# A Mamba and attention hybrid on one core: softplus on copied, wide tiles, and layer-norm statistics moved from VectorE to ScalarE

## The chip, the core and the metric

The kernel runs on one core of a Trainium2 chip. The core has five engines that each work through their own list of instructions in order: TensorE (PE; its weight loads have a row PEld), VectorE (DVE), ScalarE (ACT), GpSimd (POOL) and SyncE (SP, which here only issues transfers). They meet at semaphores. The metric is the device time of one execution in microseconds (us).

## The reference, cut to what matters

The input x is 8 images of 384 channels and 32 x 32 = 1024 positions, in float32. Two layers follow each other for each image.

```
# layer 0, for the image read forward and backward
u, z   = split(x_norm @ in_proj.T)
u      = silu(causal_conv4(u))
dt, B, C = split(u @ x_proj.T)                 # 24, 16 and 16 columns
delta  = softplus(dt @ dt_proj.T + dt_bias)
h[t]   = exp(delta*A) * h[t-1] + (delta*u) * B # 16 states for each channel
y      = (sum over states of h*C + u*D) * silu(z)
x      = x + res * (scale*(fwd + bwd) @ out_proj.T + sigmoid(conv3x3(x_norm)) * x_norm)
# layer 1, tokens t of 384 channels
t = t + causal_attention(layernorm(t))
t = t + feed_forward(layernorm(t))             # exact GELU, Kronecker-factored weights
```

The change concerns three places of it: the softplus that makes `delta`, the product `delta*u`, and the mean and variance of the two layer norms.

## The kernel before, in words

**Tiles and stages.** A half of an image is 512 positions; a tile of 128 x 512 is 128 channels over a half. An image takes four scan steps (`STEPS`: direction and half), and each step 12 units (3 blocks of 128 channels by 4 groups of states), so 48 units an image. In a unit the 128 partitions hold 32 channels by 4 states, and the four quarters of the channel block lie beside each other. One unit in `scan` is: GpSimd multiplies `hs = du * br` over 128 x 2048; ScalarE makes four tiles `da = exp(delta * A)` of 128 x 512 into five PSUM buffers (`DAS`); VectorE runs four scans over them and, in 8 of 12 units, multiplies each by `cr`; in the other units (`POOL_C`) the scans end in `hs` and GpSimd does one product with `cr`; TensorE sums the states with `sel` into the PSUM tile `y`. A small ScalarE copy (`carry`) keeps the state where a half ends.

**What feeds the scans.** `norm_in` loads x, normalizes it into the tile `xn` and projects it; `raw_gate` projects the gate from the same `xn`; `conv_tokens` makes `uc`; `prepare` (line 954) then works for one or two steps at a time. It makes `xd` by a matmul, and for each channel block and step a matmul `rates` of 128 x 512 into PSUM; `store` (line 989) takes the softplus of it, out of PSUM into a transit tile `tmp`, multiplies `uc` by it in place, and stores both to DRAM (`dd`, `db`), from which the scans load them replicated (`dl`, and `du` in a buffer of `hs`). `uc` itself has been stored to `ud` before. Tiles `tmp` are 15 shared transit buffers of 128 x 512 (`TMP`): inputs, projections on their way to DRAM, loads of `ud`, `yd`, `zs` and `lx`, and outputs. There are 17 calls of `prepare`: three for the first image, two for each other.

**Layer 1.** `project` (line 1147) sums the layer-0 result of 128 tokens in PSUM and copies it into `t1`. `token_norm` (line 1175) makes the statistics of one to four tiles of 128 tokens x 384 with `bn_stats` and `bn_aggr` on VectorE, then `rstd` and `-mean*rstd` on ScalarE; `normed` applies them. `attention` and `feed_forward` each begin with it, and `attention` ends each tile with a VectorE operation that adds its result to `t1`. That is 128 tiles of statistics in all, in 34 calls. Layer 1 of an image runs beside the scans of the next image; that of the last image is the tail.

**What sets the order.** No engine call is issued where it stands. The class `Plan` records every operation with a due time (in units) and a `rush` that moves it ahead. `Plan.order` (line 326) then goes through them with a cost table of its own: for each engine it takes, among the operations whose inputs and buffers are there by these costs, the one with the least due time less rush. It thereby fixes each engine's list, the buffer of every tile and the place of every activation-table load. An operation with a `batch` is kept together with others of its table. Where TensorE has too little work by these costs in a window of 3.413 us, measured against `KEEP`, `_fill` adds matmuls of a zero operand onto `y` (rows `y<-zero,ident`), which change nothing in the sum. The constants `FIRST`, `SECOND`, `OTHERS`, `LAYER1`, `LAYER1_7` and `PROJECT` are due times of the stages of each image. On the chip each list runs in order, whatever comes late.

Nearly all rows have line 494, where the recorded calls are issued, so rows are told apart by their tiles.

Of the kernel before, what the change touches and what calls it, by code (L numbers as in the profile page):

```python
# [30 lines left out]
P = 128  # L31
HB = 512
STEPS = [(1, 1), (1, 0), (0, 0), (0, 1)]
POOL_C = (2, 5, 8, 10)
POOL_END = (1, 3, 6, 8, 10)
TMP = 15
WTS = 2
REPS = 4
RUSH = 1.61
START = -16.0  # L40
LATER = -8.0
LATER_US = 36.0


FIRST = (2.72, 6.32, 10.68, 12.81, 18.74, 20.85)
SECOND = (22.85, 0.56)
OTHERS = (
    (3.96, 9.04, 14.9, 17.84, 20.11, 24.16, 30.75, 28, 43.27, 52.42),
    (3.99, 9.04, 15.17, 17.84, 20.3, 24.1, 30.14, 30.73, 43.27, 52.45),
    (3.99, 8.8, 14.02, 17.77, 20.08, 25.25, 30.19, 27.95, 42.89, 51),  # L50
    (3.99, 9.04, 14.9, 17.84, 19.59, 24.12, 30.52, 30.81, 42.97, 52.39),
    (3.99, 8.7, 15.25, 17.84, 20.1, 24.57, 29.82, 28, 43.27, 52.42),
    (3.99, 8.21, 14.9, 17.77, 20.1, 24.12, 30.52, 26.96, 43.27, 51.49),
    (3.82, 8.84, 15.11, 17.55, 20.38, 24.12, 29.69, 27.74, 41.51, 52.45),
)
BURST = 8.31
PROJECT = (2.31, 2.01, 2.15, 1.76, 2.22, 1.78, 2.15, 2.22, 0.91)
LAYER1 = (
    (38.52, 47.93, 60.93, 69.79, 84.06),
    (38.04, 48.09, 60.67, 69.2, 83.95),  # L60
    (38.63, 48.04, 61.04, 69.31, 84.17),
    (38.33, 47.57, 60.93, 69.59, 84.06),
    (41.08, 45.96, 60.93, 69.71, 84.06),
    (38.16, 48.76, 60.73, 69.67, 83.84),
    (44.98, 47.51, 53.66, 70.69, 74.67),
)
LAYER1_7 = (39.27, 42.31, 50.52, 59.01, 62.44, 70.84, 71.42, 76.4, 81.79)
HASTE = 25.1
FREE = ["w", "da", "w", "da"]
EXPS = -0.37  # L70
SCAN = (-1.43, -1.16, -0.47, -0.43, -0.26, 0.17, 0.01, 1.1, 0.64)
DU_AHEAD = 2.82
DL_AHEAD = 2.15
DLS = 5
DAS = 5
class _Op:
# [21 lines left out]
class Plan:  # L98
# [7 lines left out]
    }  # L106
    SWITCH = 1.4
    LOOSE = ("w", "tmp", "wt")
    HURRY = 7.14
    PATIENCE = 1.81  # L110
    TAIL = dict(tensor=0.21, vector=0.117, scalar=0.14, gpsimd=0.1, sync=0.1)
    RAW = 0.07
    NEXT = 0.01
# [5 lines left out]
    LANES = 8  # L119
    GATE = 3.413  # L120
    WARM, COLD = 0.8, 0.45
    KEEP = 0.8
    FAR = 1 << 24

    def __init__(self, nc, tc):
# [372 lines left out]
def conv_attn_kernel(  # L498
# [283 lines left out]
    def norm_in(b, h):  # L782
        xt = load_x(b, h)
        win = heavy("win", b)
        yield
        padded = plan.tile(l0, [P, NC, HR, WP], "xn")
        xn = xn_t[b, h] = padded[..., :W]
        ms = bank()
        msi = ms.rearrange("p (r w) -> p r w", w=W)
        for cc in range(NC):  # L790
            plan.scalar.square(xn[:, cc], xt[cc].rearrange("p (r w) -> p r w", w=W))
            plan.tensor.matmul(msi, ones, xn[:, cc], start=cc == 0, stop=cc == NC - 1)

        plan.scalar.activation(ms, ms, AF.Ln, bias=eps[:, 0:1], scale=1.0 / C)
        plan.scalar.activation(ms, ms, AF.Exp, scale=-0.5)
        for cc in range(NC):
            plan.vector.scalar_tensor_tensor(
                xn[:, cc], xt[cc].rearrange("p (r w) -> p r w", w=W), v_norm[:, cc : cc + 1],
                msi, ALU.mult, ALU.mult,
            )  # L800
        plan.vector.memset(padded[:, :, :, W:], 0.0)
        at = 1 + (h * HR + 1) * WP
        for cc in range(NC):
            plan.sync.dma_start(
                xq[cc * P : (cc + 1) * P, at : at + HR * WP],
                padded[:, cc].rearrange("p r w -> p (r w)"),
            )
        yield
        for m in range(NC):
            pu = bank()  # L810
            for cc in range(NC):
                plan.tensor.matmul(
                    pu.rearrange("p (r w) -> p r w", w=W),
                    win[:, cc, m * P : (m + 1) * P], xn[:, cc],
                    start=cc == 0, stop=cc == NC - 1,
                )
            u = tmp()
            plan.scalar.copy(u, pu)
            plan.sync.dma_start(up[m * P : (m + 1) * P, UP + h * HB : UP + (h + 1) * HB], u)
            if b == 0 and h == 1:  # L820
                if m == 0:
                    uc_t[b, 0] = plan.tile(l0, [P, NC, HB], "uc", 2)
                acc = uc_t[b, 0][:, m]
                plan.vector.tensor_scalar(
                    acc, u, cv[:, m, KT - 1 : KT], v_cb[:, m : m + 1], ALU.mult, ALU.add
                )
                for k in range(1, KT):
                    to = acc[:, : HB - k]
                    plan.vector.scalar_tensor_tensor(
                        to, u[:, k:], cv[:, m, KT - 1 - k : KT - k], to, ALU.mult, ALU.add  # L830
                    )
            yield
# [121 lines left out]
    def prepare(b, steps):  # L954
# [31 lines left out]
            )  # L986
            return pd

        def store(i, cc, pd):
            dl = tmp()  # L990
            plan.batch = ("softplus", b, steps[0])
            plan.scalar.activation(dl, pd, AF.Softplus, bias=v_dtb[:, cc : cc + 1])
            plan.batch = None
            du = uc_t[b, steps[i]][:, cc]
            eng.tensor_mul(du, du, dl)
            for kd, t in zip(kept[i], (dl, du)):
                plan.sync.dma_start(kd[cc * P : (cc + 1) * P], t)


        for si in steps:  # L1000
            ud = ud_t[b, si] = plan.tile(dram, [C, HB], "ud", 8)
            for cc in range(NC):
                plan.sync.dma_start(ud[cc * P : (cc + 1) * P], uc_t[b, si][:, cc])
        yield

        for cc in range(NC):
            plan.rush = BURST * (cc > 0)
            pds = [rates(i, cc) for i in range(len(steps))]
            plan.rush = BURST
            for i, pd in enumerate(pds):  # L1010
                store(i, cc, pd)
            plan.rush = 0.0
        yield

    y_t = {}
# [131 lines left out]
    def project(b, h, t1, lo=0, hi=HB):  # L1147

        yz = [yz_t[b, h, lo, cc] for cc in range(NC)]
        wout = heavy("wout", b)  # L1150
        lx = []
        for cc in range(NC):
            lx.append((tmp()[:, : hi - lo], reps()[:, : hi - lo]))
            plan.sync.dma_start(lx[cc][0], lx_t[b, h][cc * P : (cc + 1) * P, lo:hi])
            plan.sync.dma_start(lx[cc][1], xv[b, :, cc, h * HB + lo : h * HB + hi])
        yield
        for i in range((hi - lo) // P):
            cols = slice(i * P, (i + 1) * P)
            po = bank()
            for cc in range(NC):  # L1160
                plan.tensor.matmul(
                    po[:, :C], yz[cc][:, cols], wout[:, cc], start=cc == 0, stop=False,
                    skip_group_check=True,
                )
            for cc in range(NC):
                for k in range(2):
                    plan.tensor.matmul(
                        po[:, cc * P : (cc + 1) * P], lx[cc][k][:, cols], ident, start=False,
                        stop=cc == NC - 1 and k == 1, is_transpose=True, skip_group_check=True,
                    )  # L1170
            plan.scalar.copy(t1[:, h * NT + lo // P + i], po[:, :C])
            yield


    def token_norm(t1, ti0, nt):

        mv = plan.tile(l1, [P, NT, 2], "mv")[:, :nt]
        for i in range(nt):
            st = plan.tile(l1, [P, nc.vector.BN_STATS_DIM], "st", 2)
            plan.vector.bn_stats(st, t1[:, ti0 + i])  # L1180
            plan.vector.bn_aggr(mv[:, i], st)
        nrm = plan.tile(l1, [P, 2, NT], "nrm", 2)[:, :, :nt]
        plan.scalar.activation(nrm[:, 0], mv[:, :, 1], AF.Ln, bias=eps[:, 1:2])
        plan.scalar.activation(nrm[:, 0], nrm[:, 0], AF.Exp, scale=-0.5)
        minus = plan.tile(l1, [P, NT], "minus", 2)[:, :nt]
        plan.scalar.activation(minus, nrm[:, 0], AF.Identity, scale=-1.0)
        for i in range(nt):
            plan.scalar.activation(
                nrm[:, 1, i : i + 1], mv[:, i, 0:1], AF.Identity, scale=minus[:, i : i + 1]
            )  # L1190
        return nrm

# [5 lines left out]
        )  # L1198
        return xt

    kv_t = {}

    def attention(b, t1, t0, n, end=False):
        if b not in kv_t:
# [4 lines left out]
        k_all, v_all = kv_t[b]  # L1209
        half = slice(t0, t0 + n)  # L1210
        tile0, nt = t0 // P, n // P
        nrm = token_norm(t1, tile0, nt)
        yield
        if end:
            xT = plan.tile(l0, [P, NQ * HB], "hs", 5)[:, : NC * n]
# [50 lines left out]
        for i in range(nt):  # L1266
# [46 lines left out]
            for j in range(ti + 1):  # L1313
# [2 lines left out]
                    start=j == 0, stop=j == ti,  # L1316
                )
            plan.vector.scalar_tensor_tensor(
                t1[:, ti], pa[:, :C], sm[:, 6:7], t1[:, ti], ALU.mult, ALU.add
            )  # L1320
            yield

    def feed_forward(b, t1, t0, n, direct=False):
        tile0, nt = t0 // P, n // P
        nrm = token_norm(t1, tile0, nt)
        yield

        xT = plan.tile(l1, [P, NF // 2, HB], "gl")[:, :NC, :n]
# [97 lines left out]
    for b in range(NB):  # L1426
# [32 lines left out]
            local_branch(b, 1, v[8], v[9])  # L1459

        t1 = plan.tile(l1, [P, L // P, C], "t1")
        for si, (d, h) in enumerate(STEPS):

            parts = ((0, HQ), (HQ, HB)) if last and si == 3 else ((0, HB),)
# [98 lines left out]
```

## Time and profile before

| | us |
|---|---|
| median of 3 runs (least and most) | 2996.16 (2993.01, 2999.89) |
| the profiled execution, its own time | 2996.29 |
| its span, first to last instruction | 2994.5 |
| PE busy, of it the zero matmuls | 2748.8, 428.1 |
| DVE busy | 2662.6 |
| POOL busy | 2505.5 |
| ACT busy, of it table loads | 2225.2, 207.8 |

The profile has the busy time of each engine, groups of instructions by tiles with their count and mean duration, and the idle time before a group with what ended it ("idle before"). Tiles are written output<-input. A windowed view gives the same busy times for a stretch of the span. PEclk is the granted TensorE clock as a share of full speed. One matmul of this kernel in float32 leaves two records, so 810 zero matmuls are 1620 rows.

### The profile page before, as it was taken

The numbers are of one execution on the slowest core, as the hardware profiler recorded it, in microseconds if no ns is written. First come the engines' busy times: TensorE is split into PE (matmuls) and PEld (weight loads), VectorE is DVE, ScalarE is ACT, GpSimd is POOL, SyncE is SP. The second block draws the span as 40 slices with busy tenths as digits, with TensorE's granted clock in tenths as the row PEclk, the third lists the DMA queues.
The fourth block names the chain that finished last, engine by engine and source line by source line (L and its number), as shares of the span: only waits on it lengthen the run. The fifth ranks groups of instructions, "written<-read, shape, count | busy, mean of one in ns | idle before, by whom it ended". The sixth has DMA issues, their size and how long they took to land. (4 is left out here: it accounts for less than half of the span.)

```text
span 2994.5 us, 40605 instructions
## 1 busy us (share of the span) xinstructions
PE 2748.8 (92%) x12560; PEld 1245.8 (42%) x12560; DVE 2662.6 (89%) x3443; ACT 2225.2 (74%) x4166; POOL 2505.5 (84%) x692
## 2 busy tenths in 40 slices
PE   8779789999999889999999998999999998998899
PEld 4334244443444334343444434343343434444455
DVE  5799779898999899998999989999899989999971
ACT  4666567778697887878787786877778786777674
POOL 3899788698888888899988888889789889999840
PEclk9989899999999999999999999999899999999999
DMA  6778886668767687687867686676776778543510
GB/s 205 274 266 259 299 277 226 210 239 272 231 226 250 237 268 230 224 271 233 267 201 245 215 294 208 214 259 232 261 235 216 263 248 256 181 153 124 175 55 11
DMA packets 371490, 674.54 MB, mean 225 GB/s; under 512 B 44640, under 2 KB 73640, under 8 KB 371272
## 3 DMA queue, kind: packets, MB, share of 16 engines
q1 hardware_dynamic: 371144, 671.83, 67.6%
q8 instruction: 99, 1.62, 0.2%
q14 instruction: 119, 0.97, 0.1%
q0 software_dynamic: 128, 0.11, 0.0%
HBM read 505.60 MB, written 166.18 MB: 224 GB/s over the span
## 5 line engine op out<-in xcount | busy, mean ns | idle before, releaser
L494 POOL TENSOR_TENSOR hs<-hs,br 128x2048 f32<-128x2048 f32 (+2 forms) x399 | 1739.7, 4378 | 245.7 <-PE y L494 136.3
L494 ACT ACTIVATE da<-dl,nega 128x512 f32<-128x512 f32 (+1 forms) x1584 | 1040.5, 678 | 270.6 <-DVE hs L494 237.2
L494 POOL TENSOR_TENSOR hs<-hs,cr 128x2048 f32<-128x2048 f32 (+1 forms) x137 | 599.6, 4377 | 130.3 <-DVE hs L494 75.9
L494 DVE TENSOR_TENSOR_SCAN da<-da,carry,hs 128x512 f32<-128x512 f32 (+1 forms) x532 | 631.0, 1221 | 66.3 <-POOL hs L494 48.7
L494 DVE TENSOR_TENSOR hs<-da,cr 128x512 f32<-128x512 f32 (+1 forms) x1036 | 658.5, 666 | 2.1
L494 DVE TENSOR_TENSOR_SCAN da<-da,hs 128x512 f32<-128x512 f32 x504 | 595.0, 1217 | 38.9 <-ACT da L494 28.2
L494 PE MATMUL y<-hs,sel 128*32 128x512 f32 (+1 forms) x3168 | 427.3, 606 | 41.8 <-POOL hs L494 37.5
L494 PE MATMUL y<-zero,ident 128*128 128x256 f32 x1620 | 428.1, 394 | 0.0
L494 PEld LDWEIGHTS y<-zero,ident 128*128 128x128 f32 x1620 | 291.0, 193 | 160.1 <-issue 128.8
L494 DVE TENSOR_TENSOR_SCAN hs<-da,hs 128x512 f32<-128x512 f32 x264 | 307.0, 1208 | 51.0 <-ACT da L494 49.7
L494 DVE TENSOR_TENSOR_SCAN hs<-da,carry,hs 128x512 f32<-128x512 f32 (+1 forms) x284 | 325.8, 1191 | 12.6 <-ACT da L494 11.7
L494 PE MATMUL w<-xn,wt 128*128 128x512 f32 x576 | 268.0, 607 | 3.4 <-ACT tmp L494 1.7
L492 ACT ACT_TABLE_LOAD x162 | 207.8, 1283 | 2.9
L494 PE MATMUL w<-v,p 128*128 128x384 f32 x562 | 198.4, 499 | 3.9 <-ACT p L494 2.5
L494 PEld LDWEIGHTS y<-hs,sel 128*32 128x32 f32 x3168 | 90.4, 111 | 259.1 <-issue 136.4
L494 ACT COPY carry<-da 128x1 f32<-128x1 f32 x532 | 77.5, 161 | 152.6 <-DVE hs L494 151.4
L494 PE MATMUL w<-q,fc1s 32*128 32x512 f32 (+1 forms) x396 | 161.2, 679 | 28.2 <-ACT gl L494 13.4
L494 ACT COPY gl<-w 128x384 f32<-128x384 f32 (+2 forms) x317 | 160.3, 537 | 30.5 <-PE w L494 30.0
L494 PEld LDWEIGHTS w<-xn,wt 128*128 128x128 f32 x576 | 105.9, 193 | 142.9 <-issue 107.3
L494 PE MATMUL w<-rep,cit 96*32 96x512 f32 x1152 | 151.4, 639 | 4.6 <-ACT gl L494 2.8
L494 PE MATMUL y<-tmp,ddiag 128*128 128x512 f32 (+1 forms) x198 | 115.6, 669 | 43.5 <-DVE tmp L494 19.4
L494 PEld LDWEIGHTS w<-v,p 128*128 128x128 f32 x562 | 103.5, 192 | 90.3 <-ACT p L494 19.5
(187 smaller groups left out, 3349.2 us busy)
## 6 DMA issues: line engine op xcount, KB each, us to landing
hs<-db SPq DMA_DIRECT2D x372, 256.0 KB, 4.7
dl<-dd SPq DMA_DIRECT2D x372, 256.0 KB, 4.2
rep<-up SPq DMA_DIRECT2D x180, 257.5 KB, 4.2
rep<-xq SPq DMA_DIRECT2D x192, 222.4 KB, 4.8
br<-bd SPq DMA_DIRECT2D x124, 256.0 KB, 4.5
cr<-bd SPq DMA_DIRECT2D x124, 256.0 KB, 4.8
ud<-uc SPq DMA_DIRECT2D x96, 256.0 KB, 4.4
dd<-tmp SPq DMA_DIRECT2D x96, 256.0 KB, 4.0
```

The source lines that it names most:

```text
L492: self.nc.scalar.preload_act_table_set(table)
L494: op.call(*args, **{k: self._bind(v) for k, v in op.kw.items()})
```

## The change

1. In `prepare` the result of `rates` is no longer read by the softplus. ScalarE copies it with its bias (Identity) into a tile `dts` for each step, 128 x 1536 for the three channel blocks. When they are there, one softplus for each step runs in place over 128 x 1536, one product with `uc` over 128 x 1536 follows on GpSimd (VectorE in the first call), and `dd` and `db` are stored with one transfer of 768 KB each; `ud` too goes out in one transfer in place of three.
2. `dts` lies in the buffers of `xn`, of which there are now two; the transit buffers go from 15 to 11.
3. The layer-norm sums are made as the rows are written: `project`'s copy becomes an Identity with an accumulated output `sums`, and the VectorE operation that ends a tile of `attention` gets one too. `token_norm` scales `sums` to minus the mean (one small VectorE operation), and gets the variance from a ScalarE Square with that bias and an accumulated output, one for each tile. `bn_stats`, `bn_aggr` and the operation for `minus` go.
4. Rush, due times, and the planner's `HURRY`, `PATIENCE` and `KEEP` have other values.

Instructions in the two built programs that differ in number: VectorE 128 `bn_stats` and 128 `bn_aggr` go, 34 scalings come, 64 operations get an accumulated output, three products become one. ScalarE: 96 softplus become 32, and 96 Identities, 128 Squares come; 34 `minus` go; table loads 163 to 161. GpSimd: 93 products become 31. SP: 288 stores become 96. TensorE: zero matmuls 810 to 909.

```diff
-TMP = 15
+TMP = 11
-RUSH = 1.61
+RUSH = 1.34
...
-FIRST = (2.72, 6.32, 10.68, 12.81, 18.74, 20.85)
-SECOND = (22.85, 0.56)
+FIRST = (4.68, 8.72, 11.21, 12.81, 18.81, 20.85)
+SECOND = (20.62, 0.56)
...
-BURST = 8.31
+BURST = 7.56
...
-    KEEP = 0.8
+    KEEP = 0.79
...
-        padded = plan.tile(l0, [P, NC, HR, WP], "xn")
+        padded = plan.tile(l0, [P, NC, HR, WP], "xn", 2)
...
-        def store(i, cc, pd):
-            dl = tmp()
-            plan.batch = ("softplus", b, steps[0])
-            plan.scalar.activation(dl, pd, AF.Softplus, bias=v_dtb[:, cc : cc + 1])
-            plan.batch = None
-            du = uc_t[b, steps[i]][:, cc]
-            eng.tensor_mul(du, du, dl)
-            for kd, t in zip(kept[i], (dl, du)):
-                plan.sync.dma_start(kd[cc * P : (cc + 1) * P], t)
...
-            for cc in range(NC):
-                plan.sync.dma_start(ud[cc * P : (cc + 1) * P], uc_t[b, si][:, cc])
+            plan.sync.dma_start(ud.rearrange("(cc p) t -> p cc t", p=P), uc_t[b, si])
...
+        dts = [
+            plan.tile(l0, [P, NC * HR * WP], "xn", 2)[:, : NC * HB].rearrange(
+                "p (cc t) -> p cc t", cc=NC
+            )
+            for _ in steps
+        ]
         for cc in range(NC):
-            plan.rush = BURST * (cc > 0)
             pds = [rates(i, cc) for i in range(len(steps))]
-            plan.rush = BURST
             for i, pd in enumerate(pds):
-                store(i, cc, pd)
-            plan.rush = 0.0
+                plan.set = Plan.SETS[AF.Exp] if quick else None
+                plan.scalar.activation(dts[i][:, cc], pd, AF.Identity, bias=v_dtb[:, cc : cc + 1])
+                plan.set = None
+            yield
+
+        plan.rush = BURST
+        for i in range(len(steps)):
+            plan.batch = ("softplus", b, steps[0])
+            t = dts[i].rearrange("p cc t -> p (cc t)")
+            plan.scalar.activation(t, t, AF.Softplus)
+            plan.batch = None
+        for i, si in enumerate(steps):
+            du = uc_t[b, si]
+            eng.tensor_mul(du, du, dts[i])
+            for kd, t in zip(kept[i], (dts[i], du)):
+                plan.sync.dma_start(kd.rearrange("(cc p) t -> p cc t", p=P), t)
+        plan.rush = 0.0
...
-            plan.scalar.copy(t1[:, h * NT + lo // P + i], po[:, :C])
+            ti = h * NT + lo // P + i
+            plan.scalar.activation(
+                t1[:, ti], po[:, :C], AF.Identity, accum_out=sums_t[b][:, ti : ti + 1]
+            )
...
-    def token_norm(t1, ti0, nt):
-        mv = plan.tile(l1, [P, NT, 2], "mv")[:, :nt]
+    def token_norm(b, t1, ti0, nt):
+        mean = plan.tile(l1, [P, NT], "mean", 2)[:, :nt]
+        plan.vector.tensor_scalar_mul(mean, sums_t[b][:, ti0 : ti0 + nt], -1.0 / C)
+        var = plan.tile(l1, [P, NT], "var", 2)[:, :nt]
         for i in range(nt):
-            st = plan.tile(l1, [P, nc.vector.BN_STATS_DIM], "st", 2)
-            plan.vector.bn_stats(st, t1[:, ti0 + i])
-            plan.vector.bn_aggr(mv[:, i], st)
+            sq = plan.tile(l1, [P, C], "xt", 2)
+            plan.scalar.activation(
+                sq, t1[:, ti0 + i], AF.Square, bias=mean[:, i : i + 1],
+                accum_out=var[:, i : i + 1],
+            )
...
-        plan.scalar.activation(nrm[:, 0], mv[:, :, 1], AF.Ln, bias=eps[:, 1:2])
+        plan.scalar.activation(nrm[:, 0], var, AF.Ln, bias=eps[:, 1:2], scale=1.0 / C)
...
             plan.vector.scalar_tensor_tensor(
-                t1[:, ti], pa[:, :C], sm[:, 6:7], t1[:, ti], ALU.mult, ALU.add
+                t1[:, ti], pa[:, :C], sm[:, 6:7], t1[:, ti], ALU.mult, ALU.add,
+                accum_out=sums_t[b][:, ti : ti + 1],
             )
```

The due times of `OTHERS`, `PROJECT`, `LAYER1` and `LAYER1_7` are cut: most move by less than one unit, a few by up to three, and one entry of the last whole image, that of the end of its second feed-forward, from 74.67 to 84.99.

## The prediction

> **What bounds the kernel now.** I read the busy times first, then the span by stretches, then the waits of the busiest engine, then the groups that the change removes, then one softplus episode in order of time.
>
> ```profile
> span 2994.5 us, 40605 instructions
> PE 2748.8 (92%) x12560; PEld 1245.8 (42%) x12560; DVE 2662.6 (89%) x3443; ACT 2225.2 (74%) x4166; POOL 2505.5 (84%) x692
> ```
>
> Four engines are near full, so the average decides nothing. The busy times by stretches (PE, PEld, DVE, ACT, POOL):
>
> ```profile
> 0.00:598.90 598.90, 515.40 (x2145) 220.63 (x2146) 481.24 (x602) 391.46 (x682) 462.65 (x144) 0.94 0.75 252
> 598.90:2694.90 2096.00, 1959.87 (x9024) 875.25 (x9023) 1972.16 (x2481) 1637.11 (x3030) 1870.22 (x495) 0.97 0.71 237
> 2694.90:2844.70 149.80, 132.15 (x635) 68.10 (x634) 142.45 (x213) 105.78 (x249) 135.79 (x40) 0.95 0.46 149
> 2844.70:2994.40 149.70, 141.39 (x760) 81.79 (x758) 66.79 (x150) 90.86 (x207) 36.87 (x16) 1.00 0.11 33
> ```
>
> I call 598.9 to 2844.7 the middle (2245.8 us). There DVE is busy 1972.2 + 142.5 = 2114.6 us, 94.2%; PE 93.2%, but 301.7 us of it (270.24 + 31.48 in the stretches' rows of the zero operand) are zero matmuls; POOL 89.3%; ACT 1742.9 us, 77.6%. VectorE bounds the middle, with GpSimd close behind. The start (DVE 80%) and the tail (DVE 45%) are bound otherwise. VectorE's waits from 598.9 to 2694.9:
>
> ```profile
> DVE hs L494 <- ACT da L494: 42.9, 21, 6.3
> DVE da L494 <- ACT da L494: 28.0, 14, 5.7
> DVE tmp L494 <- PE y L494: 22.0, 9, 8.1
> DVE da L494 <- POOL hs L494: 12.4, 8, 2.6
> ```
>
> Most of what VectorE does wait for there is an exponential, 70.9 us. The groups concerned:
>
> ```profile
> L494 DVE BATCH_NORM_STATS2 st<-t 128x6 f32<-128x384 f32 x128 | 68.3, 548 | 5.8 <-ACT t L494 5.7
> L494 DVE BATCH_NORM_AGGREGATE mv<-st 128x2 f32<-128x6 f32 x128 | 21.2, 172 | 1.3 <-ACT nrm L494 1.0
> L494 ACT ACTIVATE tmp<-w,vec 128x512 f32<-128x512 f32 x96 | 62.2, 685 | 31.5 <-PE w L494 31.0
> L494 ACT ACTIVATE uc<-uc 128x1536 f32<-128x1536 f32 x64 | 93.5, 1482 | 2.5 <-DVE uc L494 2.2
> L494 POOL TENSOR_TENSOR uc<-uc,tmp 128x512 f32<-128x512 f32 x93 | 115.0, 1271 | 3.5 <-ACT tmp L494 3.4
> ```
>
> One softplus episode, ScalarE and then VectorE in order of time:
>
> ```profile
> 1380.04 1.28 ACT L492 ACT_TABLE_LOAD   x1
> 1381.33 1.26 ACT L494 ACTIVATE tmp<-w,vec 128x512 f32<-128x512 f32 x2
> ...
> 1383.67 1.26 ACT L494 ACTIVATE tmp<-w,vec 128x512 f32<-128x512 f32 x2 [0.22 <-PE w L494]
> 1385.86 1.26 ACT L494 ACTIVATE tmp<-w,vec 128x512 f32<-128x512 f32 x2 [0.93 <-PE w L494]
> 1387.14 1.28 ACT L492 ACT_TABLE_LOAD   x1
> 1388.43 0.69 ACT L494 ACTIVATE da<-dl,nega 128x512 f32<-128x512 f32 x1
> ...
> 1389.16 1.22 DVE L494 TENSOR_TENSOR_SCAN hs<-da,hs 128x512 f32<-128x512 f32 x1 [4.77 <-ACT da L494]
> ```
>
> For 8.4 us ScalarE makes no exponential, partly because each pair of softplus waits for TensorE (two PSUM banks `w`). The five `da` buffers run dry and VectorE stands for 4.77 us.
>
> **The change, part by part.** All sums are against the profiled execution, 2996.29 us, which equals the median (2996.16).
>
> A. Statistics off VectorE. In the middle the rows that touch `st` (both kinds) are busy 64.4 + 6.6 = 70.9 us; they go. 34 scalings at 144 ns (the row of `sm` scalings) come, 4.9 us, of which 82% lie in the middle: 4.0. 64 `attention` endings get an accumulated output. No VectorE row of before shows one; ScalarE's have a second instruction of 194 ns. Ends: nothing, or 64 x 0.194 = 12.4 us; I take the shortest VectorE row on 128x1, 0.144: 9.2 us, 7.5 in the middle. Net -59.4 (ends -66.9 and -56.7). [...]
>
> B. Softplus episodes. Of the two for each image, one is followed by a VectorE wait of over 4 us: 4.59, 6.31, 4.77, 4.62, 5.73 and 5.60 in the middle, 31.6 in all. Afterwards an episode is 1.28 + 2 x 1.48 (the row of the wide Silu) + 1.28 = 5.5 us, with nothing to wait for from TensorE between, as the Identities come before the load. 2.9 us less, six times: -17 (ends -31.6 and 0). The planned order has now and then a stray Identity or GELU copy between the loads, which is why I don't take more.
>
> C. Work added to ScalarE. Identities 96 x 0.681 (row `uc<-w,vec`) = +65.4; softplus 32 x 1.482 - 62.2 = -14.8; Squares 128 x (0.587 + 0.194) = +100.0, where 0.587 is the exponential row of 691 ns for 512 columns less the 104 ns that lie between the rows `p` of 512 and 384 columns (678 and 574), and 0.194 the accumulator read; 64 more reads +12.4; `minus` 34 x 0.204 = -6.9; two table loads -2.6. Sum +153, in the middle (75% of the span) +115: 1858 of about 2195 us, 85%. The other waits of VectorE for exponentials are 70.9 - 31.6 = 39 us. If they grow as ScalarE's free share shrinks, 22.4% to 15.4%, they become 57: +18 (ends 0 and +60, if Squares, which stand four to a call, act like softplus episodes).
> [...]
>
> D. What of it reaches the end. A, B and C make -58.4 on VectorE. GpSimd then has 2006 - 7 (its 93 products of 115.0 become 31 of 3.41, by 4.54 for 2048 columns: -9.4 in all) in about 2195 us, 91%, and waits on released buffers. I take a quarter of the relief as lost to the next engine: +14.6 (ends 0 and +58).
>
> E. Start. Before, the first softplus began at 40.39, its product at 41.11, and the last `db` store was issued at 45.31; GpSimd's first product waited for it until 51.18. Now three Identities end at about 44.5 (third matmul's result came at 43.79), then a table load that was hidden before (1.28), a softplus of 1.48, a VectorE product of some 1.7 to 2.1 (three of 0.692) and one transfer of 768 KB: about 4 us later, and up to 3 more by the landing of such transfers (4.3 to 7.4 us against 4.2). Taken +5 (ends 0 and +8).
>
> F. Tail. VectorE was not the limit. From the last row to the norm: before 0.55 + 0.17; now an accumulator read 0.19, a scaling 0.14 and two Squares 1.56, +1.2 us in each of three calls after 2900, less `minus`: +3 (ends 0 and +8).
>
> At nothing I cost: 192 stores fewer on SP (about 0.46 us of issue each, 88 us), as the steps are prepared some 28 units before their scan; SP's order behind the wide `db` stores, which now wait for a 3.4 us product, has the same cover, and without it the loads of `cr` and `dl` that GpSimd waits for in the middle (11.4 and 9.8 us) would double, +21. Fewer `tmp`: `prepare` held six and holds none, so four fewer buffers are covered. Zero matmuls: 99 more, taken as lying in TensorE's idle time; see the second rival.
>
> Sum: -59.4 - 17 + 18 + 14.6 + 5 + 3 = -35.8, so 2960.5.
>
> **The rivals.** *Full relief*: C and D at nothing, B at its end: -66.9 - 31.6 + 8 = -90, 2906. For it: VectorE's 94%; against: GpSimd and ScalarE would both need over 86% without adding a wait.
> *TensorE holds the time* (slower): the 99 zero matmuls cost 2 x 0.263 us (270.24 / 1028 by record) each, 52 us, some 39 of it in the middle. They stand in TensorE's list and are run also where real work is already late. It decides if TensorE can't be kept busier than its 93.2%: (2092 + 39)/0.932 = 2286, +41, and with E and F 3045; halfway, 3020. For it: GpSimd's longest wait in the middle is for TensorE (`hs` on `y`, 93.2 us). Against: single slices of 75 us have PE at 99%.
> *ScalarE paces the scans* (slower or same): C at +60 and D's loss of half the rest: 3000 to 3010.
> *No effect*: other waits of VectorE fill what it is relieved of: 2996 with E and F to 3004.
>
> **How the numbers follow.** About 0.2% (6 us) is what a measurement of this kernel can tell from no change. Main case 0.51 (2935 to 2985); full relief 0.15 (2895 to 2935); TensorE 0.16 (3003 to 3045); ScalarE 0.11; no effect 0.07. Faster 0.66, same 0.10, slower 0.24. From 2912 to 3022 leaves out half of full relief and the worse half of TensorE's case, under 0.2 in all.
>
> **What would show it.** Right: no `st` rows; DVE about 2580 us and still 93% or more in the middle; softplus episodes of about 5.5 us and no VectorE wait over 3 us behind them; ACT near 2380; an accumulator read on DVE; first GpSimd product of the scans near 56. Wrong: DVE below 91% of the middle with waits for `da` above 70 us (C), PE above 96% with `hs` on `y` above 93 us (TensorE), or new waits of GpSimd for loads (the transit buffers). The forecast fails if the lists put Identities and Squares where exponentials were due.

## The result and the profile after

The changed kernel takes 3079.55 us (3071.79 to 3083.82), the kernel before 2998.02 us beside it: a ratio of 1.0269, 95% interval 1.0240 to 1.0297. The forecast of 2960 us had the wrong sign, and the result lies outside its range, 2912 to 3022. The profiled execution of the changed kernel took 3071.79 us by its own time, 75.5 us more than that of before.

Its span and busy times, and the four stretches (PE, PEld, DVE, ACT, POOL, then the clock, the DMA share and GB/s):

```profile
span 3070.0 us, 40698 instructions
PE 2793.0 (91%) x12758; PEld 1274.7 (42%) x12758; DVE 2675.8 (87%) x3283; ACT 2335.2 (76%) x4482; POOL 2496.1 (81%) x630
```

```profile
0.00:598.90 598.90, 508.76 (x2185) 223.61 (x2186) 497.69 (x602) 414.14 (x725) 481.72 (x135) 0.96 0.77 255
598.90:2694.90 2096.00, 1951.65 (x8957) 874.76 (x8955) 1908.00 (x2274) 1673.62 (x3191) 1791.61 (x431) 0.97 0.71 232
2694.90:2844.70 149.80, 136.62 (x607) 65.68 (x604) 145.96 (x178) 113.74 (x216) 139.38 (x32) 0.97 0.43 139
2844.70:3070.00 225.30, 195.95 (x1017) 110.65 (x1015) 124.16 (x232) 133.68 (x352) 83.40 (x35) 0.96 0.20 64
```

VectorE has 160 instructions fewer, and is busy for 13 us more. The rows of the statistics on VectorE and ScalarE say why:

```profile
L494 DVE TENSOR_SCALAR mean<-sums 128x4 f32<-128x4 f32 x30 | 82.7, 2757 | 6.6 <-ACT t L494 6.5
L494 DVE DVE_READ_ACCUMULATOR t<-w,sm,t 128x1 f32 x63 | 5.2, 83 | 0.0
L494 DVE TENSOR_SCALAR mean<-sums 128x2 f32<-128x2 f32 x4 | 1.1, 278 | 4.2 <-ACT t L494 4.1
L494 ACT ACTIVATE xt<-t,mean 128x384 f32<-128x384 f32 x128 | 77.6, 608 | 58.2 <-DVE mean L494 58.0
L494 ACT ACTIVATION_READ_ACCUMULATOR xt<-t,mean 128x1 f32 x128 | 24.4, 191 | 0.0
```

The scaling of four numbers for each partition was costed at 144 ns. Over 128x4 it takes 2757 ns in the mean, and all 34 of them take 83.8 us; the Squares wait 58.0 us for them. The durations lie far apart: 145 ns at the least, 2315 in the median, 12334 at the most. What they wait for is seen when VectorE and GpSimd are laid beside each other in order of time (start, duration, instruction). First VectorE:

```profile
1477.63 2.46 DVE L494 TENSOR_TENSOR_SCAN da<-da,carry,hs 128x512 f32<-128x512 f32 x2
1480.00 4.33 DVE L494 TENSOR_SCALAR mean<-sums 128x4 f32<-128x4 f32 x1
1484.25 1.27 DVE L494 TENSOR_TENSOR hs<-da,cr 128x512 f32<-128x512 f32 x2
...
2866.86 12.33 DVE L494 TENSOR_SCALAR mean<-sums 128x4 f32<-128x4 f32 x1
```

Then GpSimd:

```profile
1479.79 9.01 POOL L494 TENSOR_TENSOR hs<-hs,br 128x2048 f32<-128x2048 f32 x2 [1.08 <-DMA tmp<-ud]
...
2862.90 4.77 POOL L494 TENSOR_TENSOR hs<-hs,br 128x1024 f32<-128x1024 f32 x2
2867.54 2.43 POOL L494 TENSOR_TENSOR hs<-hs,cr 128x1024 f32<-128x1024 f32 x1
2869.84 9.32 POOL L494 TENSOR_TENSOR hs<-hs,br 128x1024 f32<-128x1024 f32 x4
```

At 1480.00 a GpSimd product has just begun; two products take 9.01 us, so the first ends at about 1484.3, and there the scaling ends. At 2866.86 it outlasts the product that runs (to 2867.67) and five more that stand without a gap behind it, to 2879.19. Of the 34 scalings, 26 took more than 0.4 us; each of these began while a GpSimd product ran and ended within 0.15 us of the end of one. Of the eight short ones, six began while none ran, and two in the last 0.23 us of one.

The softplus episodes did shrink, as here, where two wide softplus stand between the loads (5.7 us from the start of the first load to the end of the second):

```profile
1361.18 1.28 ACT L492 ACT_TABLE_LOAD   x1
1362.47 2.86 ACT L494 ACTIVATE xn<-xn 128x1536 f32<-128x1536 f32 x2
1365.23 0.32 ACT L494 COPY carry<-da 128x1 f32<-128x1 f32 x4
1365.57 1.28 ACT L492 ACT_TABLE_LOAD   x1
```

Over the 17 episodes the mean of this time fell from 8.95 to 6.48 us. VectorE's longest waits at the six episodes that the prediction counted fell from 31.6 us to 16.9 in all (16.7 in the first experiment below); one of them is still 6.26 us.

### The profile page after: what moved, and what is told of

It is laid out like the page before. It is cut to its first block, busy times and chain, and to the rows that moved or that the text cites. A ratio compares the mean times of both kernels' runs of the same rounds, so it can differ in the third digit from the quotient of the medians.

```text
span 3070.0 us, 40698 instructions
## 1 busy us (share of the span) xinstructions
PE 2793.0 (91%) x12758; PEld 1274.7 (42%) x12758; DVE 2675.8 (87%) x3283; ACT 2335.2 (76%) x4482; POOL 2496.1 (81%) x630
## 5 line engine op out<-in xcount | busy, mean ns | idle before, releaser
L494 PE MATMUL y<-zero,ident 128*128 128x256 f32 x1818 | 476.4, 395 | 0.0
L494 PEld LDWEIGHTS y<-zero,ident 128*128 128x128 f32 x1818 | 328.4, 193 | 185.9 <-issue 149.7
L494 PE MATMUL w<-xn,wt 128*128 128x512 f32 x576 | 275.9, 620 | 12.9 <-ACT tmp L494 4.6
L494 PE MATMUL w<-q,fc1s 32*128 32x512 f32 (+1 forms) x396 | 154.6, 645 | 14.0 <-ACT tmp L494 5.3
L494 PE MATMUL y<-tmp,ddiag 128*128 128x512 f32 (+1 forms) x198 | 109.2, 635 | 47.8 <-DVE tmp L494 30.4
L494 PE MATMUL w<-wt,tmp 128*128 128x384 f32 x378 | 139.9, 505 | 13.8 <-ACT t L494 10.5
L494 PE MATMUL w<-rep,cit 96*32 96x512 f32 x1152 | 140.3, 609 | 1.9 <-ACT gl L494 0.6
```

The source lines that it names most:

```text
L494: op.call(*args, **{k: self._bind(v) for k, v in op.kw.items()})
```

## The experiments

Two theories at the start. *Held scaling*: the small scaling waits on VectorE for GpSimd's products, and everything behind it waits too; without that the change is a small gain. *Lists*: the new due times, the extra zero matmuls or ScalarE's added work make the loss, and the scaling's long rows only show time in which VectorE would have stood anyway.

In the experiments marked "lists kept" the order on every engine, the buffers and the table loads are those of the kernel that they start from; only what an entry of a list issues is changed. The diffs show the main lines, some of them in short.

**The scaling in pieces of one column** (the changed kernel, lists kept).

```diff
-        plan.vector.tensor_scalar_mul(mean, sums_t[b][:, ti0 : ti0 + nt], -1.0 / C)
+        def columns(to, src, by):
+            for i in range(nt):
+                nc.vector.tensor_scalar_mul(to[:, i : i + 1], src[:, i : i + 1], by)
+        plan.add("vector", columns, "tensor_scalar_mul",
+                 (mean, sums_t[b][:, ti0 : ti0 + nt], -1.0 / C), {})
```

> The changed kernel with every engine's list as it is, but each scaling of the sums over 128x4 (34 of them) issued as 128x1 pieces of one column. Theory 'held scaling': in the changed kernel's trace each of the 34 scalings is busy until a running GpSimd product ends (82.7 us in all, 2.3 us in the median, 12.3 at most, where the scaling of 128x1 in the kernel before took 0.144), so VectorE stands; a piece of one column is not held. Then the rows come to about 0.15 us a piece (some 20 us in all), VectorE's busy time falls by about 60 us, and the time falls from 3080 by 50 to 80 us, to 3000 to 3030. Rival 'order': the other due times and the place of Identities and Squares in ScalarE's list cost the time, the held scalings only fall into waits that were there anyway: less than 20 us off, 3060 or more.

**A useless scaling in the kernel before** (lists kept): behind the last `bn_aggr` of each of the 34 norms VectorE scales a spare tile, which nothing reads.

```diff
-            plan.vector.bn_aggr(mv[:, i], st)
+            def aggregate(to, src, last=i == nt - 1):
+                nc.vector.bn_aggr(to, src)
+                if last:
+                    nc.vector.tensor_scalar_mul(spare[:, 1, :nt], spare[:, 0, :nt], -1.0 / C)
+            plan.add("vector", aggregate, "bn_aggr", (mv[:, i], st), {})
```

> The kernel before with its lists as they are, and one useless scaling of a 128x4 tile more behind the last aggregation of each of the 34 token norms (result unused). Theory 'held scaling': the rows of the new scaling read 2 to 2.5 us in the mean, some 80 us of VectorE, and the time goes up by 45 to 80 us, to 3043 to 3078. Rival 'order': 34 x 0.15 = 5 us of work, at most 10 us more.

Measured: the pieces 2988.7 us, ratio 0.9974 (0.9963 to 0.9986), so 91 us less than the changed kernel and less than the kernel before. The useless scaling 3070.07 us, ratio 1.0236 (1.0203 to 1.0270), 75 us more than the kernel before. Their rows (count, then shortest, median and longest in ns), of the first and of the second:

```profile
L1191 DVE TENSOR_SCALAR mean<-sums x128: 121/142/155, 393.7 to 2950.4; 128x1 f32<-128x1 f32 x128
```

```profile
L1187 DVE TENSOR_SCALAR spare<-spare x34: 131/1717/11003, 389.0 to 3033.1; 128x4 f32<-128x4 f32 x30, 128x2 f32<-128x2 f32 x4
```

No piece of one column is held, though 112 of the 128 begin while a GpSimd product runs, and a scaling over 128x4 is held in either kernel. The second's rows sum to 76.2 us, and the run is 75 us longer: the hold is paid in full. The held scaling is thereby shown in both directions.

**What in it is held** (the changed kernel, lists kept): once the product of two tensors over 128x4, once a scaling of three columns and one of one.

```diff
+            nc.vector.tensor_mul(to, src, by_t[:, :nt])                  # by_t holds -1/384
...
+            for lo, hi in ((0, 3), (3, 4)) if nt == 4 else ((0, 1), (1, 2)):
+                nc.vector.tensor_scalar_mul(to[:, lo:hi], src[:, lo:hi], by)
```

> The kernel after, its lists kept; the scaling stays one instruction over 128x4 for a norm, but is a product of two tensors (sums by a tile that holds -1/384) in place of a product with a number. If being held by GpSimd belongs to the width of 128x4, the rows stay at 2.3 us in the median and the time is 3060 to 3085. If it belongs to the kind of instruction (one tensor by a number), the rows take 0.15 to 0.2 us and the time is that of the narrow scaling or a few us less, 2975 to 2992.

> The kernel after, its lists kept; each 128x4 scaling is issued as one of 128x3 and one of 128x1, each 128x2 as two of 128x1. If any scaling wider than one column is held by GpSimd, the rows of 128x3 take 2 us or more and the time is 3050 to 3085. If an odd number of columns isn't held, they take 0.15 to 0.2 us and the time is 2980 to 2995.

Measured: 3078.26 us, 1.0285 (1.0260 to 1.0309), and 3075.87 us, 1.0279 (1.0248 to 1.0310). Neither helped; the groups of the first and of the second:

```profile
L1192 DVE TENSOR_TENSOR mean<-sums,by_t 128x4 f32<-128x4 f32 x30 | 86.1, 2871 | 5.2 <-ACT t L494 5.2
```

```profile
L1191 DVE TENSOR_SCALAR mean<-sums 128x3 f32<-128x3 f32 x30 | 74.8, 2494 | 2.8 <-ACT t L494 2.8
L1191 DVE TENSOR_SCALAR mean<-sums 128x1 f32<-128x1 f32 x38 | 5.3, 142 | 6.4 <-ACT t L494 6.4
```

Neither the kind of instruction nor an odd width frees it: the scaling over 128x4 took 2.8 us in the mean, the product of two tensors over 128x4 2.9 and the scaling over 128x3 2.5. In the kernel before, two other operations were not held: `bn_stats` took 548 ns in the mean and 567 at the most, though 99 of the 128 began while a GpSimd product ran, and `hs<-da,cr` over 128x512 took 680 ns in the mean and 698 at the most, with 906 of 980 begun so. That one column isn't held is what the run of pieces shows (155 ns at the most). What sets the held ones apart from the others no run here shows.

**Due times exchanged**: the kernel before with all due times, `RUSH`, `HURRY`, `PATIENCE` and `KEEP` of the change, and the narrow-scaling kernel with those of before. Here the planner makes new lists.

> The kernel before with all the new rush, due times and planner values and nothing else of the change (15 transit tiles, statistics and softplus as before). Rival 'order': 30 us or more slower than before, 3030 or above. Theory 'held scaling' says nothing of it by itself, but if the scalings are the cause, this stays within 25 us of 2998.

> The changed kernel with the scalings in pieces of one column and the rush, due times and planner values of before. Rival 'order': 30 us or more faster than the narrow scalings with the new dues. Theory 'held scaling': within 25 us of that run, as the dues were no cause.

Measured: 3103.47 us, 1.0360 (1.0335 to 1.0384), and 3088.54 us, 1.0297 (1.0271 to 1.0323). The expectations for both fell. The due times are no part that can be costed alone: each set belongs to its own kernel, and with the other's the time grows by 108 and 100 us. What part 4 does by itself can't be had from such runs.

**No scaling at all** (the narrow-scaling kernel, lists kept). The Squares take the raw sums as bias; with a scale of -384 they make 384 times the deviation.

```diff
-            plan.scalar.activation(sq, t1[:, ti0 + i], AF.Square, bias=mean[:, i : i + 1], ...)
+            nc.scalar.activation(sq, t, AF.Square, scale=-float(C), bias=sums_column, accum_out=var_column)
-        plan.scalar.activation(nrm[:, 0], var, AF.Ln, bias=eps[:, 1:2], scale=1.0 / C)
+        plan.scalar.activation(nrm[:, 0], var, AF.Ln, bias=eps[:, 1:2], scale=1.0 / C**3)
+        nc.scalar.activation(mean, nrm0, AF.Identity, scale=-1.0 / C)       # -rstd/384
```

> The narrow-scaling kernel (2988.7 us) with its lists kept, without any scaling on VectorE: the Squares read the sums themselves as bias (with scale -384, so the Square sums 384*384 times the squared deviation), Ln scales by 1/384**3, and one more ScalarE Identity in each of the 34 norms makes -rstd/384. VectorE loses 128 pieces (10.7 us busy, and 10.7 us of standing before them for the last row); ScalarE gains 34 x 0.2 = 7 us. If VectorE's time is what the middle costs: 2972 to 2982. If VectorE isn't the limit any more: 2984 to 2994.

Measured: 2988.0 us, 0.9971 (0.9959 to 0.9984). VectorE is busy for 6.5 us less (2595.3 after 2601.8), which is worth nothing that can be measured.

**Fewer zero matmuls** (the narrow-scaling kernel, lists kept), for the second rival.

```diff
+                if getattr(op, "zero", False):        # a filler where the sum in y has begun
+                    self.zeros = getattr(self, "zeros", 0) + 1
+                    if self.zeros % 9 == 0:
+                        continue
```

> The narrow-scaling kernel with its lists kept, but every ninth zero matmul left out where the sum in y has begun: 815 in place of 909, about as many as before's 810. That takes 94 x 0.524 = 49 us off TensorE. If TensorE, at 94.6% of the stretch from 598.9 to 2694.9, holds the time (the second rival): 2943 to 2968, and GpSimd's waits for TensorE (hs on y, 124.6 us there) fall below 110. If zero matmuls lie in idle time of TensorE, as the prediction had it: 2983 to 2994, or more if the granted clock falls below 0.97.

Measured: 2988.62 us, 0.9971 (0.9958 to 0.9985), against 0.9974 with all of them, for 35 us less of busy TensorE. GpSimd's waits for the sums into `y` from 598.9 to 2694.9 stayed, 128.9 us after 124.6. The time of the zero matmuls did not hold the kernel, and the rival falls.

**GpSimd's products cut short** (the narrow-scaling kernel, lists kept).

```diff
+            if not quick:                                                   # quick: the first call, on VectorE
+                plan.ops[-1].call = lambda a, b, c: nc.gpsimd.tensor_mul(
+                    a[:, :, :128], b[:, :, :128], c[:, :, :128]
+                )
```

> The narrow-scaling kernel with its lists kept; GpSimd's 31 products of uc with the softplus take 128 of the 512 columns of each block, so that du is left without its factor in the rest: 31 x 3.45 = 107 us become about 28, -79 us on GpSimd, 75% of it in the middle, and the db stores can go 2.6 us earlier. If GpSimd, 88% busy in the middle, is the engine to which the relief of VectorE was lost (term D): 2925 to 2960. If not: 2982 to 2994.

Measured: 2983.83 us, 0.9963 (0.9949 to 0.9977): some 3 us, no more than the noise, for 76 us of GpSimd's busy time.

**The Squares left out** and **Silu and GELU cut short** (the narrow-scaling kernel, lists kept), for ScalarE.

```diff
+            plan.ops[-1].call = lambda *args, **kw: None                    # each Square; Ln reads a constant
...
+                nc.scalar.activation(gl[:, : NF // 6], gl[:, : NF // 6], AF.Gelu)
+            nc.scalar.activation(f[:, :512], f[:, :512], AF.Silu)
```

> The narrow-scaling kernel with its lists kept; the 128 Squares issue nothing and Ln reads a constant, so the variance is left out. ScalarE loses 128 x 0.78 = 100 us, VectorE's load is unchanged. If ScalarE's added load (term C) is what ate the relief, VectorE's waits for exponentials in the stretch from 598.9 to 2694.9 (105 us) go back towards before's 71, and the time is 2950 to 2968. If the waits come from the batches of GELU and Silu with their table loads, in which no exponential is made, the Squares matter less: 2972 to 2990.

> The narrow-scaling kernel with its lists kept; each Silu takes 512 of 1536 columns and each whole GELU 1024 of 3072, the rest is left without its function: 64 x 0.98 + 30 x 1.85 = 118 us off ScalarE, all of it in stretches without an exponential, which become 1 to 4 us shorter. VectorE stands 42 us at Silu and 59 us at GELU batches in the stretch. If these stands are where the relief went, most of some 60 to 80 us of them goes: 2930 to 2955. If VectorE is relieved only to wait elsewhere (TensorE, loads): 2975 to 2990.

Measured: 2981.78 us, 0.9956 (0.9942 to 0.9970), so some 5 us for the Squares, hardly clear of the noise; and 2963.19 us, 0.9895 (0.9882 to 0.9907), some 24 us for the parts of Silu and GELU. ScalarE's busy time fell by 71 and by 86 us. The second is less than was expected for it, but more than any other cut of one engine's work gave. VectorE's longest waits from 598.9 to 2694.9 (sum, times, longest), first in the narrow-scaling kernel:

```profile
DVE da L494 <- ACT da L494: 64.0, 34, 5.0
DVE hs L494 <- ACT da L494: 41.3, 23, 6.0
DVE da L494 <- POOL hs L494: 20.3, 10, 7.4
```

and with Silu and GELU cut short:

```profile
DVE da L494 <- ACT da L494: 44.7, 34, 3.7
DVE hs L494 <- ACT da L494: 31.6, 24, 6.1
```

**The statistics left out of the kernel before** (lists kept; mean and variance aren't computed), and **the statistics part alone in the kernel before** (lists kept; accumulated outputs, scalings of one column in the place of the last `bn_aggr`, Squares ahead of Ln).

```diff
+            plan.ops[-1].call = lambda *args: None        # each bn_stats and each bn_aggr
```

```diff
+            nc.vector.tensor_scalar_mul(mean[:, i : i + 1], total, -1.0 / C)          # for bn_aggr
...
+            for i in range(nt):                                                       # ahead of Ln
+                nc.scalar.activation(sq_t, t1_tile, AF.Square, bias=mean[:, i : i + 1],
+                                     accum_out=var[:, i : i + 1])
```

> The kernel before, its lists kept; bn_stats and bn_aggr issue nothing and Ln and minus read constants, so mean and variance are left out: 89.5 us off VectorE and nothing added anywhere. If VectorE's work bounds the middle: 2997 - 71 or somewhat less, 2920 to 2940. If about half of the statistics filled time in which no exponential was there: 2948 to 2968. If VectorE isn't the limit: 2980 to 2997. The difference to the statistics part alone is the price of the Squares on ScalarE (C).

> The kernel before, its lists kept, with the statistics part alone: accumulated outputs in project and attention, no bn_stats and bn_aggr, the 128x1 scalings at the place of a norm's last bn_aggr, the Squares just ahead of Ln; softplus, tiles and due times as before. The prediction's steps for it (A, its two thirds of C, a quarter lost) give -59 + 12 + 12 = -35: 2955 to 2970. If the statistics stood where VectorE would have waited for exponentials anyway (32 of their 69 us in the stretch lie in the longer gaps between exponentials): -8 to -25, 2972 to 2990. If the Squares delay exponentials by as much as VectorE gains: 2992 to 3005.

Measured: 2985.77 us, 0.9965 (0.9953 to 0.9978), and 3077.83 us, 1.0273 (1.0260 to 1.0286). To take the statistics from VectorE and put them nowhere gains 11 us. To put them on ScalarE, in lists that were not made for it, costs 81. The rows that left VectorE add up to 89.5 us, but its busy time fell by 63.4 only, since a row overlaps its neighbours (in the kernel before by 0.09 us in the median where two overlap); in the second kernel it fell by 50.4, and ScalarE's grew by 87.8. The stretch from 598.9 to 2694.9 with no statistics, and VectorE's waits in it:

```profile
598.90:2694.90 2096.00, 1968.44 (x9072) 876.16 (x9071) 1932.06 (x2295) 1643.14 (x3040) 1874.49 (x495) 0.97 0.72 237
```

```profile
DVE hs L494 <- ACT da L494: 51.0, 25, 6.3
DVE da L494 <- ACT da L494: 34.2, 15, 6.5
DVE tmp L494 <- PE y L494: 27.5, 15, 5.7
...
DVE t L494 <- PE w L494: 8.8, 7, 2.0
DVE sm L494 <- PE w L494: 8.0, 16, 1.1
```

VectorE is busy for 40 us less than in the same stretch of the kernel before. The waits for exponentials rose from 70.9 to 85.2 us, and those for TensorE from 26.4 to 44.3. In the kernel with the Squares put ahead of Ln the waits for exponentials are twice those of before:

```profile
DVE hs L494 <- ACT da L494: 75.4, 39, 7.7
DVE da L494 <- ACT da L494: 63.4, 30, 6.2
```

**The statistics put back on VectorE** (the narrow-scaling kernel, lists kept): in the place of each scaling, `bn_stats` and `bn_aggr` for the tiles of the norm; the Squares and accumulated outputs issue nothing.

```diff
+        def stats(to, src):
+            for i in range(nt):
+                nc.vector.bn_stats(st_t[i % 2], t1_tile)
+                nc.vector.bn_aggr(mv[:, i], st_t[i % 2])
+        plan.add("vector", stats, "tensor_scalar_mul", (mean, sums_t[b][:, ti0 : ti0 + nt]), {})
```

> The narrow-scaling kernel with its lists kept and the statistics back on VectorE: bn_stats and bn_aggr for each of the 128 tiles stand where the scalings stood, no Squares, no accumulated outputs; the softplus and the due times stay as changed. VectorE gains 89.5 - 10.7 - 5.2 = 74 us, some 55 of it in the middle; ScalarE loses 128 x 0.78 + 12 = 112 us and gains 7. If the relief of VectorE was worth what the prediction gave it (A with its part of C and D, -59 + 13 + 12 = -34): 3015 to 3035. If VectorE isn't what limits the middle: 2984 to 2996, and if ScalarE's added work cost more than VectorE's relief gave: 2965 to 2984.

Measured: 3049.7 us, 1.0175 (1.0155 to 1.0195): 61 us more for 71 us more on VectorE, though ScalarE was relieved of 69 (busy times). It is more than any expectation had. Unlike in the kernel before, up to four tiles' statistics stand there in one block (2.9 us), in lists in which the planner had counted a short operation.

**One due time put back** (the narrow-scaling kernel; the end of the second feed-forward of the last whole image 74.67 in place of 84.99), and **all five of that image**.

```diff
-    (45.23, 48.32, 50.05, 71.97, 84.99),
+    (45.23, 48.32, 50.05, 71.97, 74.67),     # and in a second run (44.98, 47.51, 53.66, 70.69, 74.67)
```

> The narrow-scaling kernel with one due time of part 4 undone: the end of the second feed-forward of the last whole image goes back from 84.99 to 74.67. Its lists stay the same up to VectorE's 2950th of 3209 instructions. From the last scan's start to the end the kernel before takes 97.5 us, the changed one 111.2 and the narrow-scaling one 110.8, with one wait of VectorE of 22.1 us for TensorE, which in that time runs feed-forward matmuls of this image. If that due time is what made the tail longer: 2971 to 2981, with a tail of about 98 us. If the tail is longer for the Squares and the scalings that every norm there now waits for: 2985 to 2993.

> The same with all five due times of that image's layer 1 as before. If only the last entry matters, the same as with the one entry, 2971 to 2981; if the other four move work of the last scans, 2980 to 3000.

Measured: 2988.01 us, 0.9978 (0.9964 to 0.9991), and 2996.5 us, 1.0008 (0.9996 to 1.0020). From the last scan's start to the end the first took 105.0 us and the second 106.1, against 110.8 with the due time of the change and 97.5 before. So that due time makes some 5 of the 13 us, but the time as a whole did not get less by it. The other 8 stay open: the kernel before has 105.3 us there with all due times of the change, and the narrow-scaling kernel 109.6 with those of before.

The best versions that were run and leave nothing out of the result, with narrow scalings or none, are 0.26 and 0.29% faster than the kernel before, and some 3% faster than the changed kernel.

## Why the prediction was wrong

The sum for the whole was -35.8 us; measured were +75.5 between the profiled executions. The starts of the first and of the last of the 1584 scans cut each execution in three:

| | predicted | changed kernel | with narrow scalings |
|---|---|---|---|
| to the first scan (before 55.8) | +5 (E) | +9.3 | +6.2 |
| first to last scan (before 2841.2) | -43.8 (A, B, C, D) | +52.5 | -24.8 |
| last scan to the end (before 97.5) | +3 (F) | +13.7 | +13.3 |

**A failed, and with it the sign.** Its step "34 scalings at 144 ns (the row of `sm` scalings) come, 4.9 us" took the price from a row of the same operation over one column. The 34 scalings, 30 of them over four columns and four over two, took 83.8 us, and the runs show the difference to be worth -91 us where it goes and +75 where it comes. The bounds of A, -66.9 and -56.7, were drawn around the accumulated output alone and had no row in them for this. The accumulated output itself, for which A had no row of VectorE, took 83 ns each, 5.3 us against 9.2 estimated. A also took the sums of rows for time: the `st` and `mv` rows add up to 89.5 us, and with the statistics left out VectorE was busy for 63.4 us less.

**D failed as well, and this shows only where the scaling is out of the way.** It gave the next engine a quarter of VectorE's relief. In the kernel before, VectorE's whole relief from the statistics, 63.4 us with nothing put in their place, was worth 11 us. So "VectorE bounds the middle", read from 94%, was wrong: a busy share says what an engine does, not that the end waits for it. From the first scan to the last, VectorE is busy for 57 us less with narrow scalings than before and waits for 46 us more, and the time between them is 24.8 us shorter.

The largest loss stands in one place. When the same scan is looked up in both traces, the narrow-scaling kernel is 5 us behind at the 155th scan and 34 us ahead at the 368th, which starts at 738.97 (part of this lead comes from a stand of before, 21.6 us at 341.2, that these lists don't have). The 369th starts only at 771.55, and the lead is down to 3 us. VectorE and GpSimd wait there:

```profile
756.97 0.75 DVE L494 SCALAR_TENSOR_TENSOR tmp<-y,gs,tmp 128x512 f32<-128x512 f32 x1 [15.56 <-DMA tmp<-zs]
766.97 9.05 POOL L494 TENSOR_TENSOR hs<-hs,br 128x2048 f32<-128x2048 f32 x2 [35.06 <-PE y L494]
```

From 714.7 to 764.0 TensorE makes no sum of states into `y`: its list has other work in that place, feed-forward and projection matmuls among it, and it is busy for 20.4 of the 25 us from 739 to 764. The longest such pause in the middle of the kernel before is 28.0 us. All 12 profiled runs with the changed lists have this stand, of 28.5 to 32.8 us between the two scans, the changed kernel too. So a lead as large as the forecast gain was lost in one place, where TensorE's list holds no sums. The two runs with exchanged due times have such stands as well, one with 15 transit buffers (two of some 40 us) and one with 11 (36 us). What share the late loads of `lx` and `zs` and the fewer buffers have in it no run shows.

Other waits can be placed too. In the kernel before, 27 of the 69.1 us of `st` and `mv` rows from 598.9 to 2694.9 begin in a gap of more than 4 us between the end of one exponential and the start of the next; there the statistics filled time in which no new exponential was ready. VectorE's waits that end between the first table load of a batch and 1 us behind its second load grew from 18.5 to 34.5 us at Silu and from 26.4 to 41.5 us at GELU. That these cost time agrees with the run that cut Silu and GELU short (24 us); that the statistics had been their cover is argued from where the rows lie, and no run tells it apart from the planner's new order.

**B was right in its mechanism.** The episodes got shorter by 2.5 us (2.9 predicted), and the six waits that it counted fell by 14.7 us (17 predicted). That this reached the end isn't shown, since waits for exponentials came back elsewhere: from 598.9 to 2694.9 they are 105.3 us with narrow scalings, 70.9 before.

**C was right in its rows and wrong as a price.** Its terms held (Identity 680 ns, wide softplus 1478, Square 608 and 191), and the rows of ScalarE add up to 152 us more, for which 153 were predicted; the busy time grew by 110, as these rows overlap too (by 0.10 us in the median). The price depends on where the Squares stand: leaving them out gained some 5 us in lists made with them, and setting them into lists made without them cost 81 in spite of VectorE's relief.

**E was too small, and F left a wait out.** The first scan begins 9.3 us later in place of 5 (61.1 to 67.1 us in the other 11 profiled runs with these lists, 5.3 to 11.3 later): the wide store of `db` is issued at 49.33 in place of 45.31 and takes 7.3 us to land (estimated up to 7.4), and the load `hs<-db` behind it is issued at 57.61 and lands at about 63, when GpSimd's first product starts (63.82, before 51.18). The tail is 13.7 us longer. The prediction looked at the norms, and the statistics part alone, in the kernel before, made the tail 3.0 us longer (100.5), as F had it. Much of the rest goes with one wait of 22 us for TensorE, 7.2 before:

```profile
2885.45 0.15 DVE L1191 TENSOR_SCALAR mean<-sums 128x1 f32<-128x1 f32 x1 [0.68 <-ACT t L494]
2907.67 0.42 DVE L494 TENSOR_TENSOR q<-w,tmp 128x256 f32<-128x256 f32 x1 [22.06 <-PE w L494]
```

In these 22 us of the narrow-scaling kernel TensorE runs mostly feed-forward matmuls of the last whole image, and 20 rows of zero matmuls (5.3 us).

Of what was costed at nothing, GpSimd's waits for loads from 598.9 to 2694.9 were 31.6 us before, 22.4 in the changed kernel and 38.0 with narrow scalings; the zero matmuls, by the run with 94 fewer, cost nothing. Of the rivals, *TensorE holds the time* came nearest to the changed kernel's time, but by luck, since its cause, the zero matmuls, was the wrong one. *ScalarE paces the scans* states 3000 to 3010, while its own terms come to about 2996; the run without Squares speaks against it, though no run left out the Identities. None of them had VectorE wait for GpSimd inside an instruction.

## What to carry to other kernels

Before a small VectorE operation is costed from a row of the same name, compare the shape as well: over one column it took 0.14 us, over three and four as long as what GpSimd had under way, 2.5 to 2.9 us in the mean. Where GpSimd is busy most of the time (81 to 84% of the span here), look at VectorE's small scalings over more than one column and its small products of two tensors, the forms that were held in this case; `bn_stats`, at most 567 ns, was not. One column at a time, or ScalarE in its place, were the ways out that were run.

In lists of fixed order, work that is taken away and work that is added have different prices. Taken from one engine, 35 to 76 us of busy time gave 0 to 11 us, and 86 us of batched activations 24. Added to lists that were made without it, 71 to 88 us cost 61 to 81 us. So a relief should be forecast at a small part of itself, unless the waits show that one engine alone is waited for. And when two traces differ, set the start of the same instruction in both beside each other along the whole span: it shows whether time was won or lost bit by bit or in one place.

## What was not expected of the hardware

In the changed kernel a held VectorE scaling mostly waited for the GpSimd product that ran: 23 of the 26 ended with it, 16 of these though the next product followed without a gap. But it wasn't always let in between two products: the longest waited for the running one and five more, 12.33 us, and the longest of the useless scalings took 11.00 us. What decides this isn't shown. The profile shows the wait as the instruction's own duration and as busy time, not as a wait with a releaser: the mean of a group, far above the least of its durations (2757 ns against 145), was the only sign. And VectorE's accumulated output is a second row (`DVE_READ_ACCUMULATOR`, 83 ns), as on ScalarE (191 to 196 ns).
